# Eviction of values, a normalisation and the order of three side steps in a fused attention and experts kernel

## The chip, the cores and the metric

The kernel runs on one core of a Trainium2 chip, in one launch. The metric is device time in microseconds of that core, the median of the runs shown. Five engines work beside each other, each through its own queue in order: TensorE (PE, with its weight loads as PEld), VectorE (DVE), ScalarE (ACT), GpSimd (POOL) and SyncE (SP), which here only issues DMAs.

## The reference

The input x is eight sequences of 512 rows of 256 numbers. Two residual blocks follow each other, each with a layer norm ahead and behind:

```python
x = x + _layernorm(attn(_layernorm(x)))
x = x + _layernorm(ffn(_layernorm(x)))
```

Attention has 16 heads of width 128 in 4 groups; the 4 heads of a group share keys and values. A fixed position table is added to queries and keys, scores are causal, and all 16 heads' results go through one output matrix:

```python
q = (x @ wq + bq).reshape(b, t, G, QPG, D).transpose(0, 2, 3, 1, 4)
kv = (x @ wkv + bkv).reshape(b, t, G, 1, 2 * D).transpose(0, 2, 3, 1, 4)
k, v = kv[..., :D], kv[..., D:]
probs = softmax(where(causal, einsum(q + pe, k + pe) / sqrt(D), -inf))
out = einsum('bgqts,bgksd->btgqd', probs, v).reshape(b, t, G * QPG * D) @ wo
```

The rows of `probs` sum to one, so a bias on `v` comes out of the product with `probs` as the same bias.

The second block sends each of the 4096 rows to its 6 best of 64 experts (gate and up products of width 176 with silu, then down), each expert taking at most 64 rows, and adds a shared expert of width 352.

## The kernel before

All data are fp32. `manual_schedule` is in force, so each engine's instructions run in the order in which the Python code issues them. The main loop runs over k = 0 to 127, that is sequence b = k // 16 and head slot s = k % 16. One turn of it works on several heads: scores of head k (`scores`, L439, four row tiles of 128 to 512 columns), softmax weights of head k (`weigh`, L457, on GpSimd), the transposition of head k − 1's weights (`turned`, L469: VectorE transposes 32 × 32 blocks, then SyncE writes them to DRAM and reads them back as `et`), the product of head k − 2's weights with the values (`mix`, L504) and the output product of head k − 3 (`project`, L520). Two tiles decide how these hold each other. `psc` (L445) comes from a pool of three PSUM buffers, `ps_s`, in turn, so the fourth score product needs the buffer of the first, which VectorE's reduction into `e` (L450) frees. `bank` (L74) hands out two PSUM buffers of `ps_m` in turn to queries, keys, values, `pav` of `mix`, the gate and the first of the two shared products `psg`; its partner `psu` is in `ps_s`.

Queries of slots from k = 4 to 95 are made for two heads at a time with seven products: `ask` (L384), `ask_sum`, `ask_rest`, `ask_fourth`, `answer` and `answer_fourth` (L430), with sums on VectorE. The third bank, `ps_b`, holds the running part and is freed by `answer_fourth`'s L433.

Beside the heads run side steps. `prepare(b + 1)` (L270) gives the next sequence's: load of x, statistics (`scales`: bn_stats and bn_aggr on VectorE, then a power on GpSimd, L102), `normal` (L280, four VectorE instructions), the exchange through DRAM that transposes rows (`turn`), `sort`, four `keys` and four `values`. The main loop takes them from the generator `ahead`: one at place M of slot 8, one in slot 9, the others at the ends of slots by a table (L1231). `feed_forward(b − 1)` (L921) gives a dictionary of steps for the previous sequence, keyed by slot and place: A after `weigh`, B after `project`, M after the query products, D after `mix`. For the first four sequences each step after slot 6 is shifted by one, so `shared_gate` and the step that makes the first hidden chunk (both driven by the generator `shared`, L846) run at 8M and 8D. `residual_sums` (L935) at 4A normalises the attention output `o`. `zeros` (L250) clears rows of a DRAM table with 128 KB DMAs from SyncE, one for each of the slots 0 to 22 until there are none left.

From k = 94 on, the experts' steps (`experts`, L787) run beside the heads of sequences 5 to 7. `EARLY` is 5, the number of sequences whose rows the experts' main pass takes. `bv_sb` (L201) holds the values' bias, broadcast to 128 partitions, and L320 adds it while it moves `pv` from PSUM to SBUF.

The side steps of one slot stand in this order in the main loop, cut to the places that matter here:

```python
side(s, "B")
if in_pairs(k + 2):
    if not quiet:
        ask(k + 2)
    ask_sum(k + 2)
side(s, "M")
if b <= EARLY and s == 8:
    next(ahead)()
if k >= 2:
    mix(k - 2)
side(s, "D")
```

Of the kernel before, what the change touches and what calls it, by code (L numbers as in the profile page):

```python
# [15 lines left out]
AF = mybir.ActivationFunctionType  # L16
# [3 lines left out]
P = 128  # L20
# [7 lines left out]
G, QPG, D = 4, 4, 128  # L28
NH = G * QPG
# [10 lines left out]
EARLY = 5  # L40
# [6 lines left out]
def sandwich_kernel(ctx, tc, x, wq, bq_t, wkv, bk_t, bv, wo, gate_wt, w_gate, w_up, w_down,  # L47
                    sh_gate_t, sh_up_t, sh_down_t, pe_t, out):
    nc = tc.nc
# [37 lines left out]
    def norm_scales(tiles, name):  # L87

        n = len(tiles)
        st = small.tile([P, n, 6], F32, tag="st", name=f"st_{name}")  # L90
        for i in range(n):
            nc.vector.bn_stats(st[:, i, :], tiles[i])
        return scales_of(st, n, name)
# [11 lines left out]
    def shifts(mv, rs, name):  # L105

        shift = small.tile([P, NI], F32, tag="shift", name=f"shift_{name}")
        nc.vector.scalar_tensor_tensor(shift, mv[:, :, 0], -1.0, rs, ALU.mult, ALU.mult)
        return shift

    def scale_on_act(dst, src, rs, shift, i):
        nc.scalar.activation(dst, src, AF.Identity, bias=shift[:, i : i + 1], scale=rs[:, i : i + 1])

    def tiles_of(t):
        return [t[:, i, :] for i in range(NI)]
# [4 lines left out]
    def normalize(dst, src, mv, rs, i):  # L120
        nc.vector.tensor_scalar(dst, src, mv[:, i, 0:1], rs[:, i : i + 1], ALU.subtract, ALU.mult)

    def on_act(dst, src):
        nc.scalar.copy(dst, src)  # L124

    def on_dve(dst, src):
        nc.vector.tensor_copy(dst, src)  # L127
# [28 lines left out]
    def as_taken(out, xt):  # L156
        return out if len(xt.shape) == 3 else out.rearrange("p (i a t) -> p i a t", i=NI, a=NI)


    with ExitStack() as part:  # L160
# [13 lines left out]
        def load(ap, shape, name):  # L174
            t = wpool.tile(shape, F32, tag=name, name=name)
            nc.sync.dma_start(out=t, in_=ap)
            return t

        def load_x(b):
            t = p2.tile([P, NI, E], F32, tag="x", name=f"x_{b}")  # L180
            rows = x[ts(b, T), :].rearrange("(i p) e -> p i e", p=P)
            if b:
                nc.sync.dma_start(out=t, in_=rows)
                return t

            for i in range(NI):
                (nc.sync, nc.scalar)[i % 2].dma_start(out=t[:, i, :], in_=rows[:, i, :])
            return t
# [9 lines left out]
        bk_sb = load(bk_t, [D, G], "bk_sb")  # L198
        bq_sb = load(bq_t, [D, NH], "bq_sb")
        pe_sb = load(pe_t, [D, T], "pe_sb")  # L200
        bv_sb = load(bv.partition_broadcast(P), [P, G * D], "bv_sb")  # L201
        wq_sb = [load(wq[:, ts(g, QPG * D)].rearrange("(c p) n -> p c n", p=P), [P, NC, QPG * D], f"wq_sb{g}")
                 for g in range(G)]
        wo_sb = load(wo.rearrange("(h d) e -> d h e", d=D), [D, NH, E], "wo_sb")
# [60 lines left out]
        NK = B * NH  # L265
# [4 lines left out]
        def prepare(b):  # L270

            s = seqs[b] = {"kt": []}

            def rows():
                s["x"] = load_x(b) if b else x_first

            def scales():
                s["scales"] = norm_scales(tiles_of(s["x"]), f"a{b}")

            def normal():  # L280
                mv, rs = s.pop("scales")
                s["xn"] = p1.tile([P, NI, E], F32, tag="xn", name=f"xn_{b}")
                for i in range(NI):
                    normalize(s["xn"][:, i, :], s["x"][:, i, :], mv, rs, i)

            def turn():
                if 0 < b <= EARLY + 1:
                    blocks = p1.tile([P, NI, NC, NI, BS], F32, tag="y", name=f"xb_a{b}")

                    def rows():  # L290
                        s["rows"] = p1.tile([P, NI, NC, NI, BS], F32, tag="y", name=f"xr_a{b}")
                        return s["rows"]

                    exchange_rows(rows, s["xn"], blocks, exr_d[0])
                    return
                s["xnt"] = p2.tile([P, NC, T], F32, tag="xnt", name=f"xnt_{b}")
                transpose_rows(s["xnt"], s["xn"], f"a{b}")

            def sort():
                s["xnt"] = p2.tile([P, NC, T], F32, tag="xnt", name=f"xnt_{b}")  # L300
                for c in range(NC):
                    nc.gpsimd.tensor_copy(as_taken(s["xnt"][:, c, :], s["rows"]), in_order(s["rows"], c))

            def keys(g):
                pk = bank([P, T], f"pk_{b}_{g}")
                for c in range(NC):
                    nc.tensor.matmul(pk, lhsT=wkv_sb[:, c, g, 0, :], rhs=s["xnt"][:, c, :],  # L307
                                     start=c == 0, stop=c == NC - 1)
                kt = p2.tile([D, T], F32, tag="kt", name=f"kt_{b}_{g}", bufs=5)
                nc.vector.scalar_tensor_tensor(kt, pk, bk_sb[:, g : g + 1], pe_sb, ALU.add, ALU.add)  # L310
                s["kt"].append(kt)

            def values(i):
                if i == 0:
                    s["v"] = p2.tile([P, NI, G * D], F32, tag="v", name=f"v_{b}")
                pv = bank([P, G * D], f"pv_{b}_{i}")
                for c in range(NC):
                    nc.tensor.matmul(pv, lhsT=s["xnt"][:, c, ts(i, P)], rhs=wkv_sb[:, c, :, 1, :],  # L318
                                     start=c == 0, stop=c == NC - 1)
                nc.vector.tensor_add(s["v"][:, i, :], pv, bv_sb)  # L320

            yield rows
            yield scales
            yield normal
            yield turn
            if 0 < b <= EARLY + 1:
                yield sort
            for g in range(G):
                yield lambda g=g: keys(g)
            for i in range(NI):  # L330
                yield lambda i=i: values(i)
# [172 lines left out]
        def mix(k):  # L504
            b, h = divmod(k, NH)
            l, g = live[k], h // QPG

            pav = bank([P, NI, NI, BS], f"pav_{k}")
            for j in range(NI):
                nc.tensor.matmul(pav[:, :, j:, :], lhsT=seqs[b]["v"][:, j, ts(g, D)],  # L510
                                 rhs=l["et"][:, :, AT[j] : AT[j] + NI - j, :], start=j == 0, stop=j == NI - 1)
            l["ao"] = p2.tile([D, T], F32, tag="ao", name=f"ao_{k}")
            ao, rows = l["ao"].rearrange("d (i a t) -> d i a t", i=NI, a=NI), pav.rearrange("d a i t -> d i a t")
            if k < NK - 1:
                on_act(ao, rows)
            else:
                on_dve(ao[:, :2], rows[:, :2])
                on_act(ao[:, 2:], rows[:, 2:])

        def project(k):  # L520
            b, h = divmod(k, NH)
# [399 lines left out]
        def feed_forward(b):  # L921
# [3 lines left out]
            l = {}  # L925
# [8 lines left out]

            def residual_sums():  # L935
                mv, rs = l.pop("scales")
                for i in range(NI):
                    normalize(l["o"][:, i, :], l["o"][:, i, :], mv, rs, i)
                for i in range(NI):
                    nc.gpsimd.tensor_add(xt[:, i, :], xt[:, i, :], l["o"][:, i, :])  # L940

# [30 lines left out]
            def go(which, n=1):  # L972
                return lambda: [next(l[which]) for _ in range(n)]

            steps = {
                "2D": copies, "3M": lambda: scales(l["o"], "o"), "4A": residual_sums,
                "5M": lambda: scales(xt, "f"), "5B": store, "6A": rows,
                "6M": turn, "7A": shared_gate, "7B": go("f"), "8A": gate,
                "8D": go("r"), "9D": go("r"),
            }  # L980
            if b < B - 2:
                steps |= {"9A": go("f"), "9B": go("f"), "11A": go("f"), "11B": go("f")}
            if b < EARLY:
                steps |= {"10A": go("r"), "10D": go("r", 2),
                          "11D": go("r", 2), "12A": go("f"), "12D": go("r", 2), "13A": go("f"), "13D": go("r", 2)}

                if b == EARLY - 1:
                    steps["6D"] = steps.pop("6M")
                    return steps
                steps["7M"], steps["7D"] = steps.pop("7A"), steps.pop("7B")  # L990
                expert, choose = steps["9A"], steps.pop("8D")
                steps["9A"] = lambda: (choose(), expert())
                return {
                    f"{int(at[:-1]) + (int(at[:-1]) > 6)}{at[-1]}": step for at, step in steps.items()}
# [160 lines left out]
        for k in range(NK):  # L1155
            b, s = divmod(k, NH)
# [49 lines left out]
                ask_fourth(k + 1)  # L1206
            if active and not finishing:
                next(routed, None)
            if k < NH + 7:
                next(zeroing, None)  # L1210
            if k in (0, 3, 6, 9):
                join_heads((k // 3 + 1) % G)
# [16 lines left out]
                ahead = prepare(b + 1)  # L1229

            for _ in range((0, 0, 0, 0, 0, 0, 1, 0, 1, 1, 2, 1, 1, 1, 2, 1)[s] if b == EARLY + 1 else 0 if b > EARLY else  # L1231
                           (0, 0, 0, 0, 0, 0, 0, 1, 0, 0, 1, 1, 2, 1, 2, 2)[s]):
                next(ahead)()
            twice = active and k > EARLY * NH + NH
            if twice and not finishing:
# [100 lines left out]
```

## Time and profile before

| what | value |
|---|---|
| three runs | 1399.25, 1399.65 and 1393.31 us |
| median | 1399.25 us |
| the profiled execution, its own time | 1400.26 us |
| its span, first to last instruction | 1398.4 us |
| granted TensorE clock, mean | 0.997 |
| busy: PE, PEld, DVE, ACT, POOL | 1361.8, 886.1, 959.5, 507.2, 475.5 us |
| instructions | 19384 |

A row of the groups or of the timeline names line, engine, operation, what is written from what, the shape and the number of instructions. In the timeline the first two numbers are start and duration in us, and a bracket at the end gives the engine's idle time ahead of the row and what ended it. A row of the waits gives the total in us, the number of waits and the longest. TensorE's instructions overlap, and their ends are modelled, so a wait shown on TensorE is shorter than the distance from start to start tells. The chain that ended last covers only the last 5 us here and tells nothing of the stages before it, so stages are read from the timeline.

### The profile page before, as it was taken

Reading aid. Unit: us, or ns where it says so; the run is one execution under the profiler, and the core shown is the slowest. Engines: PE = TensorE matmul, PEld = TensorE weight load, DVE = VectorE, ACT = ScalarE, POOL = GpSimd, SP = SyncE. Lnnn points to the kernel's source line nnn. Section 1 sums busy time; section 2 is a strip of 40 time slices with the busy share of each in tenths; the row PEclk is TensorE's granted clock in tenths of the full one; section 3 lists DMA queues with packets and bytes.
Section 4 is the critical chain, followed back from the end, with each engine's and each line's share of the span. In section 5 each row is a group of like instructions: output and inputs, shape, how many; then the busy total and the mean of one; then the engine's idle time right before and its main releaser. Section 6 shows DMA issues by size and latency. Waiting matters only on the chain. (4 is left out here: it accounts for less than half of the span.)

```text
span 1398.4 us, 19384 instructions
## 1 busy us (share of the span) xinstructions
PE 1361.8 (97%) x5478; PEld 886.1 (63%) x5478; DVE 959.5 (69%) x3396; ACT 507.2 (36%) x1444; POOL 475.5 (34%) x765
## 2 busy tenths in 40 slices
PE   8999999999999999999999999999999999999997
PEld 4666676667666676667666776655555565555664
DVE  5675588757886687668886688666666444567654
ACT  2333344224332343324432343233333333434423
POOL 4342232222422142213322232125544345355531
PEclk9999999999999999999999999999999999999999
DMA  8675577546763567446764566459998789877822
GB/s 255 161 217 167 143 191 217 152 128 168 212 181 99 162 191 207 136 120 179 215 184 110 151 199 181 111 133 300 275 298 250 223 230 262 222 210 227 272 71 69
DMA packets 167003, 261.50 MB, mean 187 GB/s; under 512 B 17245, under 2 KB 141118, under 8 KB 166894
## 3 DMA queue, kind: packets, MB, share of 16 engines
q1 hardware_dynamic: 131645, 210.17, 52.6%
q10 hardware_dynamic: 29104, 40.64, 9.3%
q0 software_dynamic: 6144, 9.44, 3.4%
q8 instruction: 44, 0.72, 0.2%
q14 instruction: 66, 0.53, 0.1%
HBM read 148.25 MB, written 111.94 MB: 186 GB/s over the span
## 5 line engine op out<-in xcount | busy, mean ns | idle before, releaser
L463 POOL TENSOR_SCALAR e<-e,recip 128x128 f32<-128x128 f32 x508 | 266.7, 557 | 697.6 <-DVE recip L460 633.3
L453 ACT ACTIVATE e<-e,least 128x128 f32<-128x128 f32 (+3 forms) x512 | 285.6, 558 | 374.0 <-DVE least L450 353.4
L446 PE MATMUL psc<-kt,qt 128*128 128x128 f32 (+3 forms) x1024 | 303.8, 436 | 4.9 <-DVE least L450 2.9
L510 PE MATMUL pav<-et,v 128*128 128x512 f32 (+3 forms) x1024 | 299.8, 436 | 7.9 <-DMA et<-ex_d 6.4
L510 PEld LDWEIGHTS pav<-et,v 128*128 128x128 f32 x1024 | 193.7, 191 | 136.0 <-issue 77.8
L450 DVE CUSTOM_DVE_ANT_0 e<-psc,mask 128x128 f32<-128x128 f32 (+3 forms) x512 | 232.4, 479 | 68.4 <-PE psc L446 59.5
L527 PE MATMUL po<-wo_sb,ao 128*128 128x256 f32 x1024 | 243.5, 381 | 0.6 <-DVE ao L127 0.6
L479 DVE STREAM_TRANSPOSE eb<-e 128x128 f32<-128x128 f32 x756 | 227.8, 364 | 8.9 <-DMA ex_d<-eb 5.9
L527 PEld LDWEIGHTS po<-wo_sb,ao 128*128 128x128 f32 x1024 | 193.1, 190 | 59.2 <-issue 29.7
L124 ACT COPY ao<-pav 128x512 f32<-128x512 f32 x128 | 74.7, 584 | 376.5 <-PE pav L510 347.7
L446 PEld LDWEIGHTS psc<-kt,qt 128*128 128x128 f32 x1024 | 165.1, 191 | 69.8 <-DVE least L450 18.9
L453 ACT ACTIVATION_READ_ACCUMULATOR e<-e,least 128x1 f32 x512 | 95.8, 187 | 0.0
L752 POOL DMA_INDIRECT y_d<-dd,idx x32 | 50.8, 1588 | 88.8 <-DMA y_d<-dd,idx 34.6
L382 PE MATMUL pq<-rows_joined,heads 128*128 128x256 f32 x276 | 75.9, 384 | 3.1 <-DVE qt L433 3.1
L382 PEld LDWEIGHTS pq<-rows_joined,heads 128*128 128x128 f32 x276 | 51.0, 190 | 33.9 <-issue 24.2
L337 PE MATMUL pq<-xnt,wq_sb 128*128 128x512 f32 x144 | 68.2, 596 | 1.2 <-DMA wq_sb<-in_wq 0.9
L307 PE MATMUL pk<-xnt,wkv_sb 128*128 128x512 f32 x128 | 59.3, 594 | 1.0 <-DMA wkv_sb<-in_wkv 0.8
L460 DVE RECIPROCAL recip<-total 128x4 f32<-128x4 f32 x128 | 22.6, 176 | 53.2 <-ACT e L453 49.7
L318 PE MATMUL pv<-wkv_sb,xnt 128*128 128x512 f32 x128 | 58.1, 592 | 0.0
L310 DVE SCALAR_TENSOR_TENSOR kt<-pk,bk_sb,pe_sb 128x512 f32<-128x512 f32 x32 | 24.0, 749 | 49.1 <-PE pk L307 49.1
L320 DVE TENSOR_TENSOR v<-pv,bv_sb 128x512 f32<-128x512 f32 x32 | 22.1, 690 | 46.1 <-PE pv L318 46.1
L127 DVE COPY ht<-pth 88x256 f32<-88x256 f32 x32 | 13.4, 418 | 50.0 <-PE pth L732 47.2
(235 smaller groups left out, 1516.7 us busy)
## 6 DMA issues: line engine op xcount, KB each, us to landing
ex_d<-eb SPq DMA_DIRECT2D x504, 160.0 KB
et<-ex_d SPq DMA_DIRECT2D x126, 640.0 KB
wgu<-in_w_gate ACTq DMA_DIRECT2D x32, 352.0 KB
wgu<-in_w_up ACTq DMA_DIRECT2D x32, 352.0 KB
wd<-in_w_down ACTq DMA_DIRECT2D x32, 352.0 KB
y<-y_d ACTq DMA_DIRECT2D x10, 512.0 KB
x<-in_x SPq DMA_DIRECT2D x7, 512.0 KB
x_d<-x SPq DMA_DIRECT2D x7, 512.0 KB
```

What stands on the lines that cost most here:

```text
L124: nc.scalar.copy(dst, src)
L307: nc.tensor.matmul(pk, lhsT=wkv_sb[:, c, g, 0, :], rhs=s["xnt"][:, c, :], start=c == 0, stop=c == NC - 1)
L318: nc.tensor.matmul(pv, lhsT=s["xnt"][:, c, ts(i, P)], rhs=wkv_sb[:, c, :, 1, :], start=c == 0, stop=c == NC - 1)
L337: nc.tensor.matmul(pq, lhsT=wq_sb[h // QPG][:, c, ts(h % QPG, D)], rhs=seqs[b]["xnt"][:, c, :], start=c == 0, stop=c == NC - 1)
L382: nc.tensor.matmul(out, lhsT=factor[0], rhs=factor[1], start=first, stop=last, skip_group_check=True)
L446: nc.tensor.matmul(psc[:, :w], lhsT=l["qt"][:, ts(i, P)], rhs=seqs[b]["kt"][h // QPG][:, :w], start=True, stop=True)
L450: nc.vector.tensor_tensor_reduce(out=e, in0=psc[:, :w], in1=mask[:, T - w :], scale=-1.0 / math.sqrt(D), scalar=BIG, op0=ALU.add, op1=ALU. ...
L453: nc.scalar.activation(e, e, AF.Exp, bias=l["least"][:, i : i + 1], scale=-1.0, accum_out=l["total"][:, i : i + 1])
L463: engine.tensor_scalar(e, e, recip[:, n : n + 1], 1.0, ALU.mult, ALU.mult)
L479: nc.vector.transpose(blocks.rearrange("p c j t -> p j c t"), l["e"][i][:, js[0] * P : (js[-1] + 1) * P].rearrange("p (j c t) -> p j c t", ...
L510: nc.tensor.matmul(pav[:, :, j:, :], lhsT=seqs[b]["v"][:, j, ts(g, D)], rhs=l["et"][:, :, AT[j] : AT[j] + NI - j, :], start=j == 0, stop=j ...
L527: nc.tensor.matmul(po[b][i // 2][:, i % 2, :], lhsT=ao[:, ts(i, P)], rhs=wo_sb[:, h, :], start=h == 0 and i % 2 == 0, stop=h == NH - 1, sk ...
```

## The change

`bv_sb` becomes a tile of 128 rows by 4 groups, loaded with the head's dimension on the partitions. `values` copies `pv` on ScalarE without a bias, and `mix` adds the group's bias column when it evicts `pav`, with an Identity activation on ScalarE instead of a copy (in the last head, half of it with an addition on VectorE). `residual_sums` normalises `o` on ScalarE for the first five sequences, with a shift made on VectorE. The shared gate and up products of the first four sequences move from place M to place B of slot 8, and the hidden chunk that follows them from D to M. The next sequence's statistics move from the end of slot 7 to place M of slot 8, so that `normal` moves from M to the end of slot 8; `turn` stays at 9B. The zeros are issued at another pace.

```diff
-        bv_sb = load(bv.partition_broadcast(P), [P, G * D], "bv_sb")
+        bv_sb = load(bv.rearrange("(g d) -> d g", d=D), [D, G], "bv_sb")
...
-                nc.vector.tensor_add(s["v"][:, i, :], pv, bv_sb)
+                on_act(s["v"][:, i, :], pv)
...
-            if k < NK - 1:
-                on_act(ao, rows)
-            else:
-                on_dve(ao[:, :2], rows[:, :2])
-                on_act(ao[:, 2:], rows[:, 2:])
+            bias, first = bv_sb[:, g : g + 1], 2 * (k == NK - 1)
+            nc.scalar.activation(ao[:, first:], rows[:, first:], AF.Identity, bias=bias)
+            if first:
+                nc.vector.tensor_scalar_add(ao[:, :first], rows[:, :first], bias)
...
                 mv, rs = l.pop("scales")
+                shift = shifts(mv, rs, f"o{b}") if b < EARLY else None
                 for i in range(NI):
-                    normalize(l["o"][:, i, :], l["o"][:, i, :], mv, rs, i)
+                    if b < EARLY:
+                        scale_on_act(l["o"][:, i, :], l["o"][:, i, :], rs, shift, i)
+                    else:
+                        normalize(l["o"][:, i, :], l["o"][:, i, :], mv, rs, i)
...
-                steps["7M"], steps["7D"] = steps.pop("7A"), steps.pop("7B")
+                steps["7B"], steps["7M"] = steps.pop("7A"), steps.pop("7B")
...
-            if k < NH + 7:
+            for _ in range((1, 1, 1, 1, 1, 1, 0, 0, 0, 0, 0, 0, 2, 2, 2, 2, 2, 2, 2, 1, 1, 1, 1)[k] if k < NH + 7 else 0):
                 next(zeroing, None)
...
             for _ in range((0, 0, 0, 0, 0, 0, 1, 0, 1, 1, 2, 1, 1, 1, 2, 1)[s] if b == EARLY + 1 else 0 if b > EARLY else
-                           (0, 0, 0, 0, 0, 0, 0, 1, 0, 0, 1, 1, 2, 1, 2, 2)[s]):
+                           (0, 0, 0, 0, 0, 0, 0, 0, 1, 0, 1, 1, 2, 1, 2, 2)[s]):
```

## The prediction

> **What bounds the kernel now.** I read the busy times first, then TensorE's waits, then the timeline around the slots that the change reorders. The page says that TensorE is busy almost all the time:
>
> ```profile
> PE 1361.8 (97%) x5478; PEld 886.1 (63%) x5478; DVE 959.5 (69%) x3396; ACT 507.2 (36%) x1444; POOL 475.5 (34%) x765
> ```
>
> TensorE's own work is the same before and after, so the change can only move its stalls: VectorE's 69% being lowered is worth nothing by itself. In the stage with paired queries (60 to 930 us) the view of TensorE's waits shows how little there is to win:
>
> ```profile
> PE pav L510 <- DMA et<-ex_d: 3.8, 4, 1.7
> PE pq L382 <- DVE qt L433: 3.1, 5, 1.3
> ```
>
> Nearly all VectorE waits lie in slot 8 of each sequence, the slot that is reordered. TensorE there, sequence 4 (b4, slot 8 starts at 680.97):
>
> ```profile
> 684.85 1.03 PE L382 MATMUL pq<-xnt,wq_sb 128*128 128x256 f32 x4
> 686.43 1.13 PE L382 MATMUL pq<-rows_joined,heads 128*128 128x256 f32 x4 [0.55 <-DVE qt L433]
> 687.39 1.88 PE L877 MATMUL psg<-xt,sg_sb 128*128 128x512 f32 x4
> 689.11 1.88 PE L877 MATMUL psu<-xt,su_sb 128*128 128x512 f32 x4
> 690.83 2.32 PE L510 MATMUL pav<-et,v 128*128 128x512 f32 x8
> 692.98 0.28 PE L446 MATMUL psc<-kt,qt 128*128 128x128 f32 x1
> ```
>
> and VectorE beside it:
>
> ```profile
> 687.01 0.39 DVE L404 TENSOR_TENSOR gxt<-pq,pe_sb 128x256 f32<-128x256 f32 x1
> 687.32 0.41 DVE L404 TENSOR_TENSOR ht<-pq,pe_sb 128x256 f32<-128x256 f32 x1
> 687.65 0.47 DVE L405 SCALAR_TENSOR_TENSOR qt<-pq,bq_sb,gxt 128x256 f32<-128x256 f32 x1
> 688.23 0.42 DVE L409 TENSOR_TENSOR gxt<-pq,gxt 128x256 f32<-128x256 f32 x1
> 688.57 1.78 DVE L121 TENSOR_SCALAR xn<-x,mv_a,rs_a 128x256 f32<-128x256 f32 x4
> 692.26 0.68 DVE L890 SCALAR_TENSOR_TENSOR gs<-gs,psg 96x512 f32<-96x512 f32 x1 [1.90 <-ACT gs L887]
> 693.05 0.68 DVE L891 SCALAR_TENSOR_TENSOR hid<-gs,psu 96x512 f32<-96x512 f32 x1
> 693.65 0.28 DVE L450 CUSTOM_DVE_ANT_0 e<-psc,mask 128x128 f32<-128x128 f32 x1
> ```
>
> See two things: the second pair of query products waits for L433, and VectorE reaches the next slot's first score (693.65) 0.67 us after TensorE started it. The statistics still sit at the end of slot 7, ahead of the e of slot 8, and their power runs on GpSimd:
>
> ```profile
> 679.97 1.41 DVE L92 BATCH_NORM_STATS2 st_a<-x 128x6 f32<-128x256 f32 x4 [0.78 <-DMA x<-in_x]
> 681.29 0.36 DVE L98 BATCH_NORM_AGGREGATE mv_a<-st_a 128x2 f32<-128x6 f32 x4
> 681.69 0.17 DVE L100 TENSOR_SCALAR ve_a<-mv_a 128x4 f32<-128x4 f32 x1
> ```
> ```profile
> 681.95 1.02 POOL L102 TENSOR_TENSOR rs_a<-ve_a,mhalf 128x4 f32<-128x4 f32 x1 [0.91 <-DVE ve_a L100]
> ```
>
> What a late VectorE costs is seen in b5, where slot 9's first e is 1.31 us behind its product. The fourth score product takes the first one's buffer (three buffers) and waits:
>
> ```profile
> 847.16 1.47 PE L446 MATMUL psc<-kt,qt 128*128 128x128 f32 x6
> 848.80 0.70 PE L446 MATMUL psc<-kt,qt 128*128 128x512 f32 x1 [0.18 <-DVE least L450]
> ```
> ```profile
> 848.47 0.27 DVE L450 CUSTOM_DVE_ANT_0 e<-psc,mask 128x128 f32<-128x128 f32 x1
> ```
>
> So TensorE resumes 0.33 us after that e starts. A matmul's modelled end hides about 0.17 us of a stall; I count stalls from start to start.
>
> **Part by part: slots 8 and 9.** In program order VectorE will do in slot 8: query adds (L404 to L409), the hidden pair L890/L891 (now at M), then the statistics, then, at the slot's end, the normalisation, which needs the power of those very statistics; then slot 9's e. Let T0 be the end of project (684.85). Shared products, now first: 687.39 to 690.83, 3.44. First query pair 0.86, and L404 starts 0.20 later (640.37 to 640.57 in b4's slot 2). L404 to the end of L409: 687.01 to 688.57, 1.56. Hidden pair: 692.26 to 693.65, 1.39; its tanh is long done by then. Statistics to normalisation: L100 starts 1.72 after L92, the power ends 1.28 after that (682.97), and 0.05 to start: 3.05, of which some 1.25 is VectorE waiting for GpSimd, with all of slot 9's e queued behind it. Normalisation 1.70 (88.13 to 89.83 in b0). Then 0.33. Sum T0 + 12.53.
>
> TensorE unhindered reaches that fourth score product at 3.44 + 0.86 + 0.86 + 2.15 (the pav group, 690.83 to 692.98) + 1.29 (three score products of 0.215, 0.43, 0.645) = T0 + 8.60. The new stall is 3.93 us. Its first 1.7 fall on pav of slot 8: the two m banks rotate, so with the shared products ahead of the queries pav takes psg's bank, and L890 frees that at T0 + 6.8 where pav could start at 5.2. The rest falls on the score product.
>
> Against it stand the stalls removed. In b4: 0.72 and 0.10 (L433, restart; the shared products now cover it) and 0.32 in slot 9 (psu's buffer, freed by L891): 1.14, so +2.8. In b1: 1.04 removed, +2.9. In b2 the statistics also waited for x and held a score product 0.8: 1.96 removed, but xt, asked for at 375.65 and landed 3.4 later by its semaphore, is now needed at 378.3: +2.6. In b3: 1.91 removed, xt 0.2 late, +2.2. In b0 there are no shared products: 85.98 + 0.20 + 1.56 + 3.05 + 1.70 + 0.33 = 92.8 against 90.3 unhindered: +2.5. In b5 the shared products stay in slot 7 and the gate's selection covers the power, but the statistics' 1.80 still comes ahead of e: +1.9 after 0.2 back in slot 8. Sum +14.9. If the waits overlap better than I read, 8; if slot 9's lateness reaches the exchange of slots 10 and 11, 19.
>
> **Values.** 32 L320 adds (690 ns) leave VectorE, 32 copies (585 ns, the row of L124 from the same bank shape) join ScalarE, 36% busy. They stand behind the exponentials and ahead of the next ones, which wait for later products anyway. VectorE's end-of-slot adds in slots 14 and 15 are followed by no stall over 0.2, so only the 0.33 wait for v at 29.6 us can go: −0.3 (−0.5 to 0). Without idle ScalarE it would be 18.7.
>
> **Bias at ao.** Nothing is removed: 127 copies become Identity with a bias. Tanh from PSUM without a pointer takes 317 ns (176 wide) and 581 (512), so 380 at 256; L1114, Identity with a bias column at 256, takes 460: +80 ns, 10.2 us of ScalarE. The Trainium skill ("ScalarE: Activation LUTs", What ACT_TABLE_LOAD costs) says that each pointer operand adds about 93 ns, 11.8 us; it speaks against the change. I take the row. On the path it is 0, since project comes a slot later; were it all exposed, +10.2 or +11.8. The last head adds 0.1.
>
> **The o normalisation.** (The heading says two; the diff moves this one, five sequences by four tiles.) VectorE loses 4 × 522 ns and gains a shift (130 ns); ScalarE gains 4 × 589 in slot 4, and ao, queued behind, is some 0.55 late (658.75 to 659.3 in b4). Its reader is in slot 5; GpSimd's adds are behind weigh until 659.2. 0, at worst 5 × 0.55 = 2.8.
>
> **bv load.** 128 packets of 2 KB (84 ns each) become 512 of 4 B. The Trainium skill ("DMA: Bandwidth & Descriptors", Rules for kernel authors) warns that a non-contiguous last dimension gives one descriptor per element. The nearest row, packets of 16 B, took 9 ns: 512 × 9 / 16 engines = 0.29 against 0.67, −0.4 at the wait for wq_sb (1.03 by starts at 12.81). The page gives no price; if SP is held as long as at 6.39 to 10.05, +1.0.
>
> **Zeros.** Six 128 KB writes leave slots 6 to 11 and join slots 12 to 18 (k = 21's goes earlier too). The SP write at 100.51 delays et of b0 slot 11, which stalls 1.85: −0.6. Two a slot in k = 16 to 18, where et is already 0.93 late: +0.5. Together −0.1 (−1 to +1.5).
>
> **Sum** 14.9 − 0.3 + 0.1 − 0.4 − 0.1 = +14.2. The profiled execution took 1400.26 (span 1398.4), 1.0 over the median of 1399.25; so 1414.5 for such an execution and 1413.4 for the median.
>
> **Rivals.** (1) Faster: the shared products cover L433's wait and x leaves VectorE's path, and the new chain does not hold TensorE. That removes 6.1 in b1 to b4 and 0.8 elsewhere: about 1392.3, at the edge of 0.5%; I count it as faster. For it speaks the visible L433 wait, the largest on VectorE; against it, VectorE would need to reach e by T0 + 8.3, not 12.2, and the power alone takes 1.0. It decides if the normalisation's chain is under 8.6. Chance 0.10. (2) Half hidden: the stall appears only where the power is uncovered, or the pav wait gives VectorE its time back fully: +3 to +6, 1403. Chance 0.12. (3) ScalarE becomes the limit for ao in slot 4: +2.8 with no slot 8 change, 1402; against it, 36% busy. Inside (2). (4) Lateness spreads into the exchange: +20, 1419 to 1421; in b3 the sort ended at 559.9 and the keys' product began at 567.7, so there is slack: 0.06, inside slower.
>
> **Numbers.** About 0.5% (7 us) is what a measurement of this kernel can tell from no change. Forecast with (4) 0.78, slower; (2) with (3) 0.12, the same; (1) 0.10, faster. The forecast's own range is 1407 to 1421 (8 to 19 for slot 8, with the bounds of the load and zeros); reaching into (2) it becomes 1398 to 1421.
>
> **What would show it.** Right: L510 waiting in slot 8 of b1 to b4 about 1.7 us for L890; L446 waiting for L450 by 2 us or more in slot 9 of b0 to b5; VectorE idle about 1.2 before L121 on rs_a; no wait for L433 in slot 8; ao near 665 ns. Wrong: those waits under 1 us together in each sequence, or a new long wait elsewhere.

## The result and the profile after

| kernel | median, us | runs | range, us | ratio to the kernel before [95% interval] |
|---|---|---|---|---|
| before | 1399.45 | 4 | 1393.31 to 1403.86 | |
| changed | 1413.05 | 4 | 1412.84 to 1414.54 | 1.0103 [1.0064, 1.0142] |
| changed, again (with the third set below) | 1411.86 | 6 | 1408.30 to 1417.58 | 1.0114 [1.0094, 1.0134] |

The change costs about 1.0%. (In the third set the kernel before took 1395.89 us, the median of 19 runs, so there the change cost 16.0 us, against 13.6 in the first comparison.) The profiled execution of the changed kernel took 1413.15 us, span 1410.9, against 1400.26 and 1398.4 before: +12.5 us of span.

The row of busy times in the page of the changed kernel, then TensorE's waits between 60 and 930 us (engine, operation, line, what released it and on which engine: us in total, times, longest):

```profile
PE 1366.5 (97%) x5478; PEld 890.6 (63%) x5478; DVE 929.9 (66%) x3349; ACT 548.1 (39%) x1496; POOL 475.6 (34%) x765
```
```profile
PE psc L446 <- DVE least L450: 14.6, 6, 2.6
PE pav L510 <- DVE qt L405: 1.9, 5, 0.4
PE pav L510 <- DMA et<-ex_d: 1.4, 3, 0.7
PE psg L876 <- DMA xt<-exr_d: 1.4, 4, 0.5
```

VectorE lost 29.6 us of work (959.5 to 929.9) and the kernel became slower. The L433 wait of 3.1 us that the kernel before showed on query products is gone. In its place stand six waits of a score product for L450, 14.6 us. PE's busy time rose by 4.7 us with the same 5478 matmuls. A stall can't do that; we come back to it.

Where the wait lies: slot 8 into slot 9 of sequence 4 (b4) in the timelines of TensorE, VectorE and GpSimd (start, duration, engine, line, in brackets the idle time before and its releaser):

```profile
694.65 1.96 PE L876 MATMUL psg<-xt,sg_sb 128*128 128x512 f32 x4 [0.49 <-DMA xt<-exr_d]
696.44 1.88 PE L876 MATMUL psu<-xt,su_sb 128*128 128x512 f32 x4
698.15 1.03 PE L382 MATMUL pq<-xnt,wq_sb 128*128 128x256 f32 x4
699.02 1.03 PE L382 MATMUL pq<-rows_joined,heads 128*128 128x256 f32 x4
700.42 2.42 PE L510 MATMUL pav<-et,v 128*128 128x512 f32 x8 [0.38 <-DVE qt L405]
702.68 1.47 PE L446 MATMUL psc<-kt,qt 128*128 128x128 f32 x6
706.78 2.07 PE L446 MATMUL psc<-kt,qt 128*128 128x512 f32 x2 [2.64 <-DVE least L450]
```
```profile
700.81 0.68 DVE L889 SCALAR_TENSOR_TENSOR gs<-gs,psg 96x512 f32<-96x512 f32 x1
701.52 0.68 DVE L890 SCALAR_TENSOR_TENSOR hid<-gs,psu 96x512 f32<-96x512 f32 x1
702.12 1.39 DVE L92 BATCH_NORM_STATS2 st_a<-x 128x6 f32<-128x256 f32 x4
703.44 0.36 DVE L98 BATCH_NORM_AGGREGATE mv_a<-st_a 128x2 f32<-128x6 f32 x4
703.83 0.17 DVE L100 TENSOR_SCALAR ve_a<-mv_a 128x4 f32<-128x4 f32 x1
705.14 1.38 DVE L121 TENSOR_SCALAR xn<-x,mv_a,rs_a 128x256 f32<-128x256 f32 x4 [1.14 <-POOL rs_a L102]
706.44 0.28 DVE L450 CUSTOM_DVE_ANT_0 e<-psc,mask 128x128 f32<-128x128 f32 x1
```
```profile
704.09 1.02 POOL L102 TENSOR_TENSOR rs_a<-ve_a,mhalf 128x4 f32<-128x4 f32 x1 [4.94 <-DVE ve_a L100]
```

Slot 9's score products begin at 702.68. VectorE reads the first of them at 706.44 because the statistics, the wait for GpSimd's power and the normalisation stand ahead of that e. TensorE issues three score products (two matmuls each), has no buffer for the fourth, and resumes at 706.78, 0.34 us after the e starts. (L876, L889, L890, L515 here are L877, L890, L891 and the ao copy of the kernel before; from start to start the wait is 2.80.)

From start to start, slots 7 to 9 grew by 3.6, 2.9, 5.1, 2.1, 4.5 and 1.9 us in b0 to b5, 20.1 together; the rest of the span gave 7.6 back.

### The profile page after: what moved, and what is told of

Read it like the earlier page. It is cut to its first block, busy times and chain, and to the rows that moved or that the text cites. A ratio compares the mean times of both kernels' runs of the same rounds, so it can differ in the third digit from the quotient of the medians.

```text
span 1410.9 us, 19395 instructions
## 1 busy us (share of the span) xinstructions
PE 1366.5 (97%) x5478; PEld 890.6 (63%) x5478; DVE 929.9 (66%) x3349; ACT 548.1 (39%) x1496; POOL 475.6 (34%) x765
## 5 line engine op out<-in xcount | busy, mean ns | idle before, releaser
L450 DVE CUSTOM_DVE_ANT_0 e<-psc,mask 128x128 f32<-128x128 f32 (+3 forms) x512 | 233.8, 479 | 148.4 <-PE psc L446 138.3
L446 PE MATMUL psc<-kt,qt 128*128 128x128 f32 (+3 forms) x1024 | 305.8, 438 | 17.0 <-DVE least L450 16.8
L515 ACT ACTIVATE ao<-pav,bv_sb 128x512 f32<-128x512 f32 x128 | 87.7, 685 | 378.0 <-PE pav L510 362.3
L446 PEld LDWEIGHTS psc<-kt,qt 128*128 128x128 f32 x1024 | 166.2, 191 | 81.1 <-DVE least L450 30.3
L382 PE MATMUL pq<-xnt,wq_sb 128*128 128x256 f32 x184 | 47.3, 380 | 0.3 <-DVE kt L310 0.3
```

The costliest lines, as they stand in the source:

```text
L382: nc.tensor.matmul(out, lhsT=factor[0], rhs=factor[1], start=first, stop=last, skip_group_check=True)
L446: nc.tensor.matmul(psc[:, :w], lhsT=l["qt"][:, ts(i, P)], rhs=seqs[b]["kt"][h // QPG][:, :w], start=True, stop=True)
L450: nc.vector.tensor_tensor_reduce(out=e, in0=psc[:, :w], in1=mask[:, T - w :], scale=-1.0 / math.sqrt(D), scalar=BIG, op0=ALU.add, op1=ALU. ...
L515: nc.scalar.activation(ao[:, first:], rows[:, first:], AF.Identity, bias=bias)
```

## Experiments

Every kernel was run beside the kernel before; times are medians and ratios are to that. Kernels of one set ran on the same chip, each set on another. The kernel before took 1397.73, 1396.72 and 1395.89 us in the three sets.

### First set: which move costs

**Statistics back at the end of slot 7**, shared products still early:

```
-  (0, 0, 0, 0, 0, 0, 0, 0, 1, 0, 1, 1, 2, 1, 2, 2)[s]
+  (0, 0, 0, 0, 0, 0, 0, 1, 0, 0, 1, 1, 2, 1, 2, 2)[s]
```


> The changed kernel with one edit undone: the next rows' statistics, power and normalisation are issued at the end of slot 7 again, not of slot 8; the shared products stay in slot 8's first half. Queue theory (TensorE in slot 9 is held by VectorE's statistics, the wait for GpSimd's power, and the first normalisation, which all stand ahead of the fourth score product's e): with them out of that queue VectorE is at that e about 3.1 us earlier, so the waits of L446 for L450 of 2.6 us in b1 to b4 fall under 0.9 us, no half clock windows in slot 9, and the time falls below the kernel before: 20 of slots 7 to 9 go, the rest of the change (-8 in the comparison of the traces) stays: 1388 to 1398 us. Rival (the shared products' move itself costs: xt and et not there, hidden's pair ahead of the e): at least half of the 20 us stays: 1403 or more, and a wait of over 1.5 us in slots 8 and 9 on xt or on L450.

**Shared products and hidden back**, statistics still late:

```
-  steps["7B"], steps["7M"] = steps.pop("7A"), steps.pop("7B")
+  steps["7M"], steps["7D"] = steps.pop("7A"), steps.pop("7B")
```


> The changed kernel with the other edit of the order undone: shared products and hidden one half slot later as before (slot 8's second half and slot 9), statistics still at the end of slot 8. Queue theory: VectorE has hidden's 1.4 us not ahead of the statistics but right after the turn, still in competition with e; the power's 1.1 us wait and the normalisation stay ahead of the fourth score product's e, so slot 9 still waits, by 2.6 less up to 1.4, 1.2 to 2.6 us per sequence, and the time is 1399 to 1410. Rival (it is the shared products' move that costs): under 1396.

**Both back** (both edits above):

> The changed kernel with both moves of the order undone, so that values' copies and bias, the o normalisation, the bias' load and the zeros' pace remain. Prediction's sum for these: -0.7 us, so 1398.5. Comparison of the traces: what lies outside slots 7 to 9 is -8 us, of which some -4 comes from half clock windows that fall elsewhere in the last two sequences; so 1391 to 1397. If these parts cost something (ScalarE's added work in slots 4 and 6), it is above 1400.

**The kernel before with both moves alone** (the two edits reversed, on the kernel before):

> The kernel before with only the two moves of the order (shared products a half slot to a slot earlier, statistics and normalisation one slot later). Queue theory with the half clock windows: slots 7 to 9 cost what the comparison showed, 15 of waits and about 5.6 of half clock, so 1414 to 1420, with L446 waits for L450 of 2.6 us in slot 9 of b1 to b4. Rival (the moves cost only because ScalarE and VectorE are busier with the other parts): under 1406.

| kernel | time, us | ratio [interval] | L446 waits for L450, 60 to 930 us |
|---|---|---|---|
| statistics back | 1393.00 | 0.9967 [0.9949, 0.9985] | 0.2 (one) |
| shared back | 1401.94 | 1.0027 [1.0013, 1.0040] | 6.2 (six) |
| both back | 1392.57 | 0.9960 [0.9943, 0.9977] | 0.2 (one) |
| both moves alone | 1416.82 | 1.0128 [1.0108, 1.0148] | 14.6 (six) |

The two moves alone reproduce the loss, with the very same 14.6 us of waits, on a kernel where ScalarE does none of the added work. So the loss is in the order. With both moves undone the rest of the change gains 0.40%. The shared products' move alone is worth nothing either way (0.9967 against 0.9960); that rival falls. The statistics' move alone costs 0.67% (1.0027 against 0.9960, 9 us), and both together 1.5% (1.0114 against 0.9960, 22 us): more than their sum.

Why more than the sum is in the trace of "shared back", VectorE in b4:

```profile
691.92 0.17 DVE L100 TENSOR_SCALAR ve_a<-mv_a 128x4 f32<-128x4 f32 x1
693.90 0.68 DVE L889 SCALAR_TENSOR_TENSOR gs<-gs,psg 96x512 f32<-96x512 f32 x1 [1.81 <-ACT gs L886]
694.69 0.68 DVE L890 SCALAR_TENSOR_TENSOR hid<-gs,psu 96x512 f32<-96x512 f32 x1
695.30 1.37 DVE L121 TENSOR_SCALAR xn<-x,mv_a,rs_a 128x256 f32<-128x256 f32 x4
```

With the shared products late, hidden comes between the statistics and the normalisation and the power is done meanwhile; moreover the shared products themselves take TensorE's time just before slot 9, so VectorE is only 1.01 us late for the fourth score product in b1 to b4, not 2.80. That is 4 × 1.79 = 7.2 of the 12 us that are missing from the sum. The others fit the half clock described below: slot 9 of "shared back" has none of it, while the two profiles of the changed kernel have three and four windows of it there.

### Second set: what in the statistics' move costs, and where the gain is

**The normalisation later still**, in slot 9 ahead of the turn:

```
             if s == 9 and b <= EARLY + 1:
                 next(ahead)()
+                if b <= EARLY:
+                    next(ahead)()
...
-  (0, 0, 0, 0, 0, 0, 0, 0, 1, 0, 1, 1, 2, 1, 2, 2)[s]
+  (0, 0, 0, 0, 0, 0, 0, 0, 0, 0, 1, 1, 2, 1, 2, 2)[s]
```


> The changed kernel with one step later still: the four normalisations are issued in slot 9 just ahead of the turn that reads them, not at the end of slot 8; statistics and power stay in slot 8, shared products in its first half. Queue theory: the fourth score product's e no longer stands behind the power's wait (1.1 us) and the normalisation (1.7 us); VectorE reaches e at about T0 + 9.7 against TensorE's T0 + 8.6, so the wait of L446 for L450 falls from 2.6 to 0.3 to 1.1 us, TensorE gets no half clock window in slot 9, and the time is 1392 to 1400; turn and sort come 2 to 4 us later, which the slack before the keys' product holds. Rival (it is the amount of VectorE's work in these slots, wherever it stands): the wait moves to another e of slot 9 and at least 10 of the 19 us stay, 1407 or more. Second rival (the turn is on the path): keys wait for the exchanged rows in slot 12, up to 4 us per sequence, over 1410.

**Statistics and power early, only the normalisation late:**

```
-            if b <= EARLY and s == 8:
-                next(ahead)()
...
-  (0, 0, 0, 0, 0, 0, 0, 0, 1, 0, 1, 1, 2, 1, 2, 2)[s]
+  (0, 0, 0, 0, 0, 0, 0, 1, 1, 0, 1, 1, 2, 1, 2, 2)[s]
```


> The changed kernel with statistics and power back at the end of slot 7 and only the normalisation left at the end of slot 8, shared products in slot 8's first half: the power's wait is taken away, and statistics' 1.8 us with it. By the prediction's sum VectorE is at the fourth score product's e at T0 + 12.5 less 3.05 = 9.4 to 9.5 against TensorE's 8.6, so 0.9 us of the 2.6 us wait stays, and the time is 1393 to 1400. Rival (the normalisation's 1.7 us in front of e is what costs): waits of 1.5 us or more stay, 1403 to 1407.

**Values alone** (the kernel before with the bias' load, the copies at L320 and the bias at ao):

> The kernel before with only the values' part of the change: copies on ScalarE in place of the additions on VectorE, the bias added in the heads' result, the bias loaded across partitions. The prediction gave these -0.6 together. In the comparison of the kernel without the two moves of the order with the one before, the gains that lie in sequences 6 and 7 (2.5 and 3.4 us, waits for et and for xg) have no zeros and no o normalisation on ScalarE near them; if they come from the values' evictions leaving VectorE, this kernel is 2 to 4 us under the one before (1394 to 1396); if from where half clock windows and loads happen to fall, within 1.5 us of it.

**Values, bias and o normalisation** (both moves undone, and the zeros at one a slot):

```
-  for _ in range((1, 1, 1, 1, 1, 1, 0, 0, ...)[k] if k < NH + 7 else 0):
+  if k < NH + 7:
```


> The changed kernel without both moves of the order and with the zeros written one in each slot as before, so values, bias and o normalisation alone. The prediction gave the zeros' pace -0.1 (-0.6 in sequence 0, slot 11, +0.5 at k = 16 to 18). The traces show 0.74 gained in sequence 0 and 1.8 in sequence 1 where et had been waited for (slots 1 and 5). If the zeros' pace is what took these waits, this kernel is 2 to 3 us over the one without the moves of the order, at 1394.5 to 1396 (ratio to before 0.998); if the other parts did, it is equal to it, 1392 to 1393.5 (ratio 0.996).

| kernel | time, us | ratio [interval] |
|---|---|---|
| normalisation in slot 9 | 1399.78 | 1.0020 [1.0006, 1.0035] |
| statistics and power early | 1390.84 | 0.9961 [0.9945, 0.9977] |
| values alone | 1395.41 | 0.9994 [0.9980, 1.0009] |
| values, bias, o normalisation | 1393.62 | 0.9976 [0.9958, 0.9993] |

*Statistics and power early* is the cleanest. The wait is gone altogether, not reduced to the 0.9 us that was expected, and the time lies under the expected 1393 to 1400, though normalisation, hidden and shared products stand where the change put them. TensorE and VectorE in b4:

```profile
683.66 2.42 PE L510 MATMUL pav<-et,v 128*128 128x512 f32 x8 [0.38 <-DVE qt L405]
685.92 2.32 PE L446 MATMUL psc<-kt,qt 128*128 128x128 f32 x8
```
```profile
684.76 0.68 DVE L890 SCALAR_TENSOR_TENSOR hid<-gs,psu 96x512 f32<-96x512 f32 x1
685.36 1.37 DVE L121 TENSOR_SCALAR xn<-x,mv_a,rs_a 128x256 f32<-128x256 f32 x4
686.65 0.28 DVE L450 CUSTOM_DVE_ANT_0 e<-psc,mask 128x128 f32<-128x128 f32 x1
```

All eight score products run as one group. The e starts 0.73 after the first score product; in the changed kernel 3.76. The difference of 3.02 is the statistics and the power's wait (702.12 to 705.14 in the changed kernel), and the fourth product, due at 1.30, has 0.23 of slack: 3.02 − 0.23 = 2.79 against 2.80 measured.

*Normalisation in slot 9* fell on its expected band's upper edge, and its first rival had a part: the wait moved. Waits of TensorE, and VectorE in slots 9 and 10 of b4:

```profile
PE psc L446 <- DVE qt L424: 3.9, 5, 0.8
```
```profile
697.64 2.19 DVE L121 TENSOR_SCALAR xn<-x,mv_a,rs_a 128x256 f32<-128x256 f32 x4
699.75 1.41 DVE L144 STREAM_TRANSPOSE xb_a<-xn 128x256 f32<-128x256 f32 x4
701.08 0.44 DVE L424 SCALAR_TENSOR_TENSOR qt<-third,bq_sb,ht 128x256 f32<-128x256 f32 x1
```

Normalisation and turn now follow one another ahead of the query addition of slot 10, whose first score products wait 0.9 to 1.1 from start to start in b0 to b4. VectorE's work does not vanish by being moved on; it needs a place with slack.

*Values*: the trace of values alone lies under the one before by 1.0 and 0.6 (b1, slots 1 and 5), 3.1 (b6, slots 4 and 5), 0.8 and 2.2 (b7, slots 4 and 6), at waits for et or xg that are gone or shorter (the last with the half-clock window that the kernel before had there). It loses 2.6 in b0's slot 11 and 2.8 in b6's slot 9, each with a half-clock window. The median shows only −0.06%, not distinct from nothing.

Most of these gains can't be put down to the values. The trace of both moves alone, which keeps the additions on VectorE, has the same slots shorter than before: by 0.6 and 0.3 in b1, 3.0 in b6 and 1.7 in b7's slot 4. Only b7's slot 6 sets old and new values apart. It took 12.7 and 12.4 us in the two traces with the old ones, each with a half-clock window, and 10.1 to 11.0 in the twelve with the new, without one. Its wait for xg does not: 1.04 and 0.76 there, up to 1.00 here. With two traces of the old values this may be chance.

With the o normalisation beside the values the gain is 0.24%, with the zeros' pace 0.40%; these intervals overlap, so what the zeros give is open.

### Third set: does any VectorE work do it, and is the power on the path

**Idle work** on the kernel with statistics back at slot 7, ahead of its normalisation, with n = 4 and n = 8 (the result is unused):

```
             mv, rs = s.pop("scales")
+            if 0 < b <= EARLY + 1:
+                extra = small.tile([P, 6], F32, tag="extra", name=f"extra_a{b}")
+                for _ in range(n):
+                    nc.vector.bn_stats(extra, pe_sb[:, :E])
```


> The kernel with statistics back at the end of slot 7 and the shared products early, plus idle work: four bn_stats of a constant (4 x 0.347 = 1.39 us of VectorE, their result unused) ahead of the normalisation in slot 8 of sequences 0 to 4. There the fourth score product had 0.23 us of slack and no wait. Queue theory: whatever the work is, TensorE waits one for one, 1.39 less 0.23 = 1.15 us in b1 to b4 (similar in b0, none in b5 beyond what it has), no half clock window in slot 9, so 5 to 7 us over the kernel without it: 1396 to 1400. Rival (it is the wait for GpSimd's power that holds TensorE, not VectorE's occupation): no wait, 1391 to 1393.

> The same with eight of them, 2.78 us: about the 3.02 by which statistics and power delay e in the changed kernel. Queue theory alone, linear: waits of 2.55 us, 5 x 2.55 = 12.8 over the kernel without idle work, 1403 to 1406. With half clock windows, which the changed kernel showed after waits of 2.64 in three of six places and the kernel with the two moves alone in four sequences of four: 3 to 8 us more, 1406 to 1413, and PEclk 0.5 in slot 9 of some sequences. If half clock does not depend on the wait's length, both doses show as many windows.

**Power covered**, the changed kernel with statistics ahead of hidden:

```
+            if b <= EARLY and s == 8:
+                next(ahead)()
             side(s, "M")
-            if b <= EARLY and s == 8:
-                next(ahead)()
```


> The changed kernel with one order turned: in slot 8 the next rows' statistics and power are issued ahead of hidden's pair (L889, L890), not behind it, so that hidden's 1.39 us run while GpSimd computes the power. Queue theory: the wait for rs_a (1.1 us before L121) goes and nothing else moves, so e is 1.1 us earlier and the wait of L446 for L450 falls from 2.6 to about 1.5 in b1 to b4, which is below what has led to half clock: 1413 less 4 x 1.1 less the windows' 3 to 5 = 1402 to 1406. Rival (the power is not on the path): same time, 1411 to 1415.

**The changed kernel again:**

> The changed kernel as it is, in the same call as the others. All theories: 1412 to 1416, waits of 2.64 us in slot 9 of b1 to b4. If half clock windows depend on where a wait falls against a fixed grid of 3.41 us, their sequences need not be the same (b0, b2, b4 in the first profile), and each costs 1.4 to 1.7 us where it falls on slot 9.

| kernel | time, us | ratio [interval] | slot 9's wait in b1 to b4, start to start |
|---|---|---|---|
| statistics back (first set) | 1393.00 | 0.9967 [0.9949, 0.9985] | 0 |
| four idle | 1398.96 | 1.0028 [1.0012, 1.0043] | 1.49 |
| power covered | 1403.67 | 1.0047 [1.0028, 1.0067] | 1.56 |
| eight idle | 1417.74 | 1.0141 [1.0122, 1.0161] | 3.34 |
| changed, again | 1411.86 | 1.0114 [1.0094, 1.0134] | 2.80 |

Both doses were larger than planned: these bn_stats, which all write one tile, don't overlap, and four took 1.80 us, eight 3.65. The four of the statistics, which write different parts of a tile, take 1.39; that the shared output makes the difference was not tested. TensorE and VectorE in b4 of the kernel with eight (its lines are four further down):

```profile
707.62 1.47 PE L450 MATMUL psc<-kt,qt 128*128 128x128 f32 x6
712.26 1.23 PE L450 MATMUL psc<-kt,qt 128*128 128x512 f32 x2 [3.17 <-DVE least L454]
```
```profile
707.06 3.65 DVE L285 BATCH_NORM_STATS2 extra_a<-pe_sb 128x6 f32<-128x256 f32 x8
710.63 1.37 DVE L121 TENSOR_SCALAR xn<-x,mv_a,rs_a 128x256 f32<-128x256 f32 x4
711.91 0.29 DVE L454 CUSTOM_DVE_ANT_0 e<-psc,mask 128x128 f32<-128x128 f32 x1
```

The e came 1.70 and 3.55 later; less the slack of 0.23 that is 1.47 and 3.32, against waits of 1.49 and 3.34. So it is one for one and the kind of work doesn't matter; the rival "only the power's wait" falls. I had also overlooked that the idle work ran in b5 too, whose wait rose by 1.67 and 3.53. With that the small dose should cost 0.96 + 4 × 1.49 + 1.67 = 8.6, and the ratios give 0.61%, 8.5 us. The large one should cost 2.92 + 4 × 3.34 + 3.53 = 19.8, and the ratios give 1.74%, 24 us. The 4 us over are no wait in slot 9.

*Power covered*: VectorE runs hidden while GpSimd works, the 1.14 wait is gone and e is 1.23 earlier. The wait falls from 2.80 to 1.56, as expected, part of it now at the third score product, which waits for hidden:

```profile
PE psc L446 <- DVE least L450: 6.2, 6, 2.1
PE psc L446 <- DVE hid L890: 2.6, 4, 0.6
```

4 × 1.23 = 4.9, but the time fell by 8.2 (1411.86 to 1403.67). Again 3 us that are no wait in slot 9.

## What is left over: the half clock

In the profiles both remainders are TensorE running at half clock, that is, at a granted clock of 0.50. Slot 9 of b0 to b5 has seven windows of 3.41 us at half clock with eight idle and one with four; with the power covered it has none, the changed kernel three and four. Windows of the second profile of the changed kernel (us, busy time and count of PE, PEld, DVE, ACT, POOL, then PEclk, DMA share, GB/s), around slot 9 of b1 and of b2:

```profile
230.30:233.70 3.40, 1.97 (x11) 1.25 (x9) 2.23 (x12) 0.69 (x1) 1.02 (x1) 1.00 0.04 12
233.70:237.10 3.40, 2.20 (x10) 1.30 (x11) 3.40 (x14) 0.99 (x4) 0.00 (x0) 1.00 0.00 0
...
387.30:390.70 3.40, 1.24 (x6) 0.57 (x4) 2.23 (x11) 0.69 (x1) 1.02 (x1) 1.00 0.02 9
390.70:394.10 3.40, 2.93 (x5) 1.24 (x6) 3.40 (x14) 1.35 (x5) 0.00 (x0) 0.50 0.02 6
394.10:397.50 3.40, 3.40 (x16) 2.66 (x17) 3.17 (x11) 2.35 (x12) 2.03 (x4) 1.00 0.72 189
```

Both have the same wait of 2.80. In b1 it is split over two windows, and in each TensorE is busy for about 2 us. In b2 most of it falls in one, TensorE is busy for 1.24 of 3.40, and the window that follows is granted 0.50: five matmuls fill 2.93 us. Slot 9 then grew by 4.0 to 4.2 us in b2, b3 and b4, and by 2.6 in b1: 1.4 to 1.6 us for a window. This is also why PE's busy time rose: its matmuls took longer. It is 1356.3 to 1359.7 us in the four profiles without half clock ahead of the last 10 us, 1366.5 in the one with five windows and 1368.4 and 1371.3 in the two with seven.

Over the profiles of the changed kernel (two), both moves alone, shared back, power covered and the two doses, slot 9 of b0 to b5:

| wait from start to start, us | places | followed by half clock |
|---|---|---|
| 0.96 to 1.57 | 13 | 0 |
| 2.05 to 2.29 | 11 | 2 |
| 2.80 to 2.92 | 13 | 9 |
| 3.34 to 3.91 | 5 | 5 |

In the changed kernel it fell on b0, b2 (two windows in a row) and b4 in the first profile, on b2, b3 and b4 in the second, and on b1 to b4 with both moves alone. The half-clock stretches between 60 us and the kernel's last 10 us lasted 3.41 us or twice that, and the stretches before and between them whole multiples of it (85.33 is 25 times 3.413, 296.96 is 87 times). So the windows lie on a fixed grid, and what a wait of 2.80 does depends on where it falls on it.

## Why the prediction was right, and where not

**The order, +14.9 predicted.** The mechanism was the one foretold: statistics, the power's wait and normalisation ahead of slot 9's first e. Statistics to normalisation was put at 3.05; taking statistics and power out moved e by 3.02. The wait at the fourth score product was foretold as about 2.2 (3.93 less 1.7) and was 2.80 (2.28 in b0, 2.1 in b5), on the line named, in all six sequences. By start to start slots 7 to 9 grew by 20.1 in the first profile and 17.6 in the second. By the medians the two moves cost 18 us on the kernel before (1.0128), and 20 and 22 on the kernel that has the rest of the change (1.0103 and 1.0114 against 0.9960).

**The pav step was wrong.** I had pav of slot 8 wait 1.7 for psg's bank, freed by L890. It waited 0.54 (0.38 shown), and for L405: it takes the bank of the pair's first query products, not psg's, which L889 still reads from 700.81 on, when pav has begun (700.42). The two banks are not handed out strictly in turn. So the total stall was 3.34, not 3.93. The normalisation, put at 1.70, took 1.30 from its start to e's; and xt, foretold late only in b2 and b3, came 0.3 to 0.7 late in b1 to b4 of the first profile, in the second by more than 0.1 only in b4 (0.6).

**The half clock was left out.** The sum priced a stall at its length. Over the forecast slots 7 to 9 cost 5.2 us in the first profile and 2.7 in the second. The half-clock windows, four at 1.4 to 1.6 us in the first (two of them in a row) and three in the second, account for all of it and for the shorter stall.

**The rest, −0.7 predicted, was mis-sized.** With both moves undone the other parts give −5.2 us (1392.57 against 1397.73; the ratio's interval gives −8.0 to −3.2). Which term was too small is open. Values alone, with their bias and its load, were put at −0.6, and the median gives −0.8, with an interval that holds zero. The o normalisation was put at 0 and the zeros at −0.1; with the first the gain is 0.24%, with both 0.40%, and the intervals overlap. I looked for stalls beside the additions of slots 14 and 15. The traces are shorter elsewhere, at waits for et and xg in b1, b6 and b7, but mostly so with the old values too.

What the load of bv gave (−0.4 predicted) can't be read either. The profile counts 511 more packets under 512 bytes, and those of 4 bytes took 9 ns each in the first 25 us, as put. But head 0's score products began at 16.4 and 17.4 us in the two traces with the old load, and at 14.9 to 17.3 in the twelve with the new. The bias at ao cost 100 ns (before, then changed):

```profile
L124 ACT COPY ao<-pav 128x512 f32<-128x512 f32 x127 | 74.3, 585 | 373.7 <-PE pav L510 347.7 <-DMA wgu<-in_w_up 23.0 <-issue 3.0
L515 ACT ACTIVATE ao<-pav,bv_sb 128x512 f32<-128x512 f32 x128 | 87.7, 685 | 378.0 <-PE pav L510 362.3
```

That is 685 against 585; the row gave 80, the Trainium skill ("ScalarE: Activation LUTs", What ACT_TABLE_LOAD costs) 93, which was nearer. As foretold TensorE waits nowhere for the ao of ScalarE. In the last head, where half of ao is an addition on VectorE, the output product's wait for ao grew from 0.6 to 1.1 us, against 0.1 foretold for that head.

**So the total, 1413.4 against 1413.05, is partly luck:** 3 to 7 us too little for the order and some 4.5 too little gain for the rest.

**Rivals.** "Faster" asked that VectorE reach e before T0 + 8.3; it didn't. With statistics and power early VectorE is in time, 0.23 us before TensorE would wait, and the kernel is faster, though only by 0.4%. "Half hidden" falls, since the wait stood in all six sequences. "Lateness spreads into the exchange" falls too: between 60 and 930 us the changed kernel has no wait of a keys' product. "ScalarE becomes the limit" falls with "both back", where ScalarE has all the added work.

**A version better than both**: statistics and power at the end of slot 7, all else as changed, 0.9961 [0.9945, 0.9977]; both moves undone is as good, 0.9960 [0.9943, 0.9977].

## What to carry over

When a step is moved on an engine that is no bottleneck, count what then stands ahead of the next read that frees a buffer for the bottleneck; its slack here was 0.23 us, and beyond that each microsecond was paid in full, five or six times. A step that ends in another engine's result (here a 1 us power) is best issued a slot before its reader, or with other work between the two. Price a stall of the matrix engine with what follows it too: two waits of 1.4 cost less here than one of 2.8, since the lost clock follows from how little TensorE did in one window of the grid.

## What was not expected of the hardware

Idle time shorter than a window is enough for half clock. The Trainium skill ("TensorE: Matmul & The Clock Gate", Part 1: The HAM clock gate) describes a free-running window of 3413 ns and a clock that drops after at least one idle window. The window's length and grid agree with these traces. The threshold doesn't: here windows in which TensorE was busy for a third of the time were enough (1.24 of 3.40 us), after waits of 2.05 to 2.80 us. Whether it happened differed between runs of one kernel, since the waits fell differently on the grid.

All fourteen profiles can be cut into windows of their grid, from 20 us to the last 10 us, and sorted by TensorE's busy share (with the modelled ends). These are the windows at full clock:

| busy share of the window | windows | followed by half clock |
|---|---|---|
| 0.41 or less | 20 | 20 |
| 0.45 to 0.65 | 61 | 6 |
| more | 5511 | 0 |

What decides in the middle row stays open.
